# Masked cross-attention of a decoder: where the query projections and the token-gather masks stand in the instruction order

## The chip, the cores and the metric

The kernel runs on one core of one Trainium2 chip. The metric is the device time of one execution in microseconds. Before the change it is 1451.39 us, the median of three runs (1450.63 to 1454.59).

## The reference, cut to what matters

The reference is a decoder of two layers over 16 sequences of 128 tokens with 256 features. The change lies in the last attention and in the hand-over to the last feed-forward part (a mixture of eight experts, each of which picks the 32 tokens of a sequence that it scores highest):

```python
# masked cross-attention, 16 heads of 64
Q = (query @ W_q);  K = (key_value @ W_k);  V = (key_value @ W_v)
scores = jnp.einsum('bhmk,bhnk->bhmn', Q, K)
scores = jnp.where(mask == 0, jnp.float32(-1e+20), scores)
attn = jax.nn.softmax(scores / np.sqrt(D_K), axis=-1)
ctx = jnp.einsum('bhmn,bhnv->bhmv', attn, V)
x = _layernorm(x + ctx @ W_o)

# experts that choose tokens: E = 8, k = 128 // 8 * 2 = 32
affinity = jnp.transpose(jax.nn.softmax(jnp.einsum('bsd,ed->bse', x, gate_w)), (0, 2, 1))
gating, idx = jax.lax.top_k(affinity, k)
x_in = x[bidx, idx]
h = jax.nn.silu(x_in @ w_gate.T) * (x_in @ w_up.T)
x_e = h @ w_down.T
out = jnp.zeros_like(x).at[bidx, idx].add(gating[..., None] * x_e)
x = _layernorm(x + out)
```

## The kernel before, in words

All sixteen sequences stay in SBUF as tiles `x[b]`, 128 tokens by 256 features. The stages run one after the other; the masked attention is `stage4`, the experts are `stage5`.

`stage4` sets its order of work by hand: it opens a block with `manual_schedule`, and inside it every engine executes its instructions in the order in which the Python code issues them. The loop runs over the sequences, `for n in range(NB)` (L1936), and is a software pipeline. In iteration n the kernel makes the scores of sequence n in two halves of eight heads (`scores(n, 0)`, `scores(n, 1)`, L1827), the exponentials of n on ScalarE (`exp`, L1846), the division by the row sums on GpSimd after a reciprocal on VectorE (`weighted`, L1851), the transposes of the weights of n-1 in four pieces (`turn_weights(n-1, 0..3)`, L1855), each copied out of PSUM by `turned` (L1860: pieces 0 and 2 on ScalarE, 1 and 3 on VectorE), the product with the values for n-1 (`attend4`, L1863), and the output projection, residual and layer norm of n-2 (`product`, `residual`, `normed`).

Two sequences share one query projection. The queries of the pair g+1 are made during pair g: `queries(g+1)` is a generator of four pieces, each of eight matmul instructions in TensorE (L1747) and one evacuation on VectorE (L1752). An iteration takes two pieces, both directly behind `scores(n, 1)`. In odd iterations `turn(g + 2)` (L1811) transposes the input of the pair after that, which must follow the last piece that reads the one buffer `xT`.

Routing for the experts rides along. `r5.turn(n-3)` (L2075) transposes a finished sequence, ScalarE copies it out, and `r5.gauge(n-3)` (L2083) multiplies it with the gate weights. `r5.choose` (L2091) is a generator that turns the affinities of eight sequences into positions; for the first eight it is stepped through in iterations 11 to 13. `r5.take(b)` (L2136) then gathers the chosen tokens of one sequence: VectorE compares an index row with the positions and writes the 0/1 mask `hot` (L2125), TensorE multiplies `x[b]` with it, ScalarE copies the result to `xin`. Takes of sequences 0 to 7 come as fillers in iterations 13, 14 and 15 (L1910), those of 8 to 15 in a loop at the end of the stage (L2036). In iterations 0 and 1 the fillers are instead the last pieces of the keys and values (L1755, L1760), copied out by ScalarE.

PSUM limits this. `ps_t` (transposes and attention products) has two buffers, and `ps_m` (query pieces, `turn`, `product`, `r5.turn`, `r5.gauge`, takes, fillers) has two buffers. `hot` has two buffers in SBUF. `stage5` uses the same function `hot` with a pool of its own for the way back (`ways`, L2145); that stage has no order written by hand, and some of its mask instructions stand already inside iteration 13 in the trace.

The heart of the iteration before the change:

```python
scores(n, 1)
if g + 1 < NB // G:
    all_of(some(asked, g + 1, queries, 2))
if last:
    normed(n - 2)
if n > 2:
    r5.turn(n - 3, small, kv.ps)
if i == 1 and g + 2 < NB // G:
    turn(g + 2)
```

Of the kernel before, what the change touches and what calls it, by code (L numbers as in the profile page):

```python
# [8 lines left out]
F32 = mybir.dt.float32  # L9
# [11 lines left out]
NB = 16  # L21
# [1697 lines left out]
class Context4:  # L1719


    G = 2
# [59 lines left out]
def all_of(parts):  # L1782
    for _ in parts:
        pass


def stage4(K, w, kv, r5, res):
# [6 lines left out]
    with ExitStack() as ctx:  # L1794
        keep = ctx.enter_context(tc.tile_pool(name="s4_keep", bufs=1))
        grp = ctx.enter_context(tc.tile_pool(name="s4_grp", bufs=2))
        work = ctx.enter_context(tc.tile_pool(name="s4_work", bufs=2))
        small = ctx.enter_context(tc.tile_pool(name="s4_small", bufs=4))
# [8 lines left out]
        G = kv.G  # L1807
# [3 lines left out]
        def turn(g):  # L1811
            xT[g] = K.new(grp, [P, KD, G * P], F32, "xT", bufs=1)
            px = K.new(kv.ps, [P, KD, G * P], F32, "ps_m")
            for k in range(KD):
                for i in range(G):
                    nc.tensor.transpose(px[:, k, i * P:(i + 1) * P], x[G * g + i][:, k * P:(k + 1) * P], K.ident)
            nc.scalar.copy(xT[g], px)
# [6 lines left out]
        def half(b, j):  # L1824
            return s[b][:, 8 * j:8 * j + 8, :]

        def scores(b, j):  # L1827
            g, at = divmod(b, G)
            mine = slice(at * P, at * P + P)
            if j == 0:  # L1830
                s[b] = K.new(work, [P, NH, P], F32, "s")
            pss = K.new(ps, [P, 2, 4, P], F32, "ps_s")
            for c in range(4):
                for i in range(2):
                    rows = slice(64 * i, 64 * i + 64)
                    nc.tensor.matmul(  # L1836
                        pss[:, i, c, :], qT[g][j][rows, c, mine], kT[g][j][rows, c, mine], start=True, stop=True,
                    )
            nc.vector.tensor_tensor(  # L1839
                half(b, j), pss.rearrange("p r c k -> p (r c) k"), hide.unsqueeze(1).to_broadcast([P, 8, P]), ALU.add,  # L1840
            )
            m[j] = K.new(small, [P, 8], F32, f"m{j}", bufs=2)
            nc.vector.tensor_reduce(m[j], half(b, j), AX.X, ALU.max, negate=True)  # L1843
            t[j] = K.new(small, [P, 8], F32, f"t{j}", bufs=2)

        def exp(b, j, which):  # L1846
            for i in which:
                at = half(b, j)[:, i, :]
                nc.scalar.activation(at, at, AF.Exp, bias=m[j][:, i:i + 1], accum_out=t[j][:, i:i + 1])  # L1849

        def weighted(b, j):  # L1851
            nc.vector.reciprocal(t[j], t[j])  # L1852
            nc.gpsimd.tensor_tensor(half(b, j), half(b, j), t[j].unsqueeze(2).to_broadcast([P, 8, P]), ALU.mult)  # L1853
# [21 lines left out]
        def product(b):  # L1875
            py[b] = K.new(kv.ps, [P, D], F32, "ps_m")
            for c in range(NC):
                nc.tensor.matmul(py[b], oT[b][:, c, :], w.o[c // 4][:, c % 4, :], start=(c == 0), stop=(c == NC - 1))  # L1878

        def residual(b):  # L1880
            r[b] = K.new(work, [P, D], F32, "r")
            nc.vector.tensor_tensor(r[b], x[b], py[b], ALU.add)
            st = K.new(small, [P, 6], F32, "ln_st")
            nc.vector.bn_stats(st, r[b])
            mv[b] = K.new(small, [P, 2], F32, "ln_mv")
            nc.vector.bn_aggr(mv[b], st)
            rs[b] = K.new(small, [P, 1], F32, "ln_rs")
            K.rsqrt(small, rs[b], mv[b][:, 1:2], 1.0, 1e-5, "ln_t")

        def normed(b):  # L1890
            nc.vector.tensor_scalar(x[b], r[b], mv[b][:, 0:1], rs[b], ALU.subtract, ALU.mult)


        asked = {}

        def some(held, at, make, n):

            if at not in held:
                held[at] = make(at)
            for _ in range(n):  # L1900
                next(held[at])
                yield

        def fillers(n):
            if n < 2:
                for _ in range((3, 100)[n]):
                    if next(kv.rest, kv) is kv:
                        break
                    yield
            for b in {13: (0, 1), 14: (2, 3, 4, 5), 15: (6, 7)}.get(n, ()):  # L1910
                r5.take(b, small, kv.ps)
                yield

        H = NB // 2
        early, late = r5.choose(0, H, small, kv.ps), r5.choose(H, NB, small, kv.ps)
# [20 lines left out]
        for n in range(NB):  # L1936
            old, last = n > 0, n > 1
            g, i = divmod(n, G)
            parts = fillers(n)
            scores(n, 0)  # L1940
            exp(n, 0, range(8))
            if last:
                product(n - 2)
                residual(n - 2)
            scores(n, 1)
            if g + 1 < NB // G:
                all_of(some(asked, g + 1, queries, 2))
            if last:
                normed(n - 2)
            if n > 2:  # L1950
                r5.turn(n - 3, small, kv.ps)
            if i == 1 and g + 2 < NB // G:
                turn(g + 2)
            if n in (11, 12, 13):
                next(early, None)
            weighted(n, 0)
            exp(n, 1, range(0, 3))
            if old:
                turn_weights(n - 1, 0)
                turned(n - 1, 0)  # L1960
            next(parts, None)
            if n in (11, 12):
                next(early)
            exp(n, 1, range(3, 6))
            if old:
                turn_weights(n - 1, 1)
                turned(n - 1, 1)
            if n > 2:
                r5.gauge(n - 3, kv.ps)
            next(parts, None)  # L1970
            if n in (11, 12):
                next(early)
            exp(n, 1, range(6, 8))
            if old:
                turn_weights(n - 1, 2)
                turned(n - 1, 2)
            next(parts, None)
            if old:
                turn_weights(n - 1, 3)
                turned(n - 1, 3)  # L1980
            weighted(n, 1)
            next(parts, None)
            if old:
                attend4(n - 1, 0)
            all_of(parts)
            if old:
                attend4(n - 1, 1)
            if n == 12:
                next(early)

            if i == 1 and g + kv.ahead < NB // G:
                kv.fetch_keys(g + kv.ahead)
            if old and n - 1 + G * kv.ahead < NB:
                kv.fetch_values(n - 1 + G * kv.ahead)
            if n == 13:
                first = load5(
                    K, 0, lambda i, shape: K.new(kv.ring, [P, 4, 2 * P], F32, "ring").rearrange("p c n -> p (c n)")
                    if len(shape) == 2 else K.new(kv.ring, [P, 4, 2 * P], F32, "ring"),
                )


        b = NB - 1
# [31 lines left out]
        first_down(1)  # L2034
        all_of(late)
        for b in range(H, NB):  # L2036
            r5.take(b, small, kv.ps)
    return first


# [22 lines left out]
class Routes:  # L2063


    def __init__(self, K, pool):
        self.K = K
        self.gw = K.load(pool, "l1f_gate_wT", [P, KD, NE], rearr="(k p) e -> p k e", p=P)
        self.aff = K.new(pool, [P, NB, NE], F32, "aff")
        self.pos = K.new(pool, [P, NB, NE], F32, "pos")  # L2070
        self.xin = K.new(pool, [P, KD, NE, NB * TOK], F32, "xin")
        self.xT, self.back = {}, []


    def turn(self, b, work, ps):  # L2075
        K, nc = self.K, self.K.nc
        pt = K.new(ps, [P, KD, P], F32, "ps_m")
        for k in range(KD):
            nc.tensor.transpose(pt[:, k, :], K.x[b][:, k * P:(k + 1) * P], K.ident)
        self.xT[b] = K.new(work, [P, KD, P], F32, "xT5", bufs=2)  # L2080
        nc.scalar.copy(self.xT[b], pt)
# [43 lines left out]
    def hot(self, b, pool):  # L2125

        K, W = self.K, [P, NE, TOK]
        hot = K.new(pool, W, F32, "hot", bufs=2)
        K.nc.vector.tensor_tensor(
            hot, K.iota[:, :TOK].unsqueeze(1).to_broadcast(W), self.pos[:, b, :].unsqueeze(2).to_broadcast(W),  # L2130
            ALU.is_equal,
        )
        return hot


    def take(self, b, work, ps):  # L2136
        K, nc = self.K, self.K.nc
        hot = self.hot(b, work)
        pg = K.new(ps, [P, KD, NE, TOK], F32, "ps_m")
        for k in range(KD):  # L2140
            nc.tensor.matmul(pg[:, k, :, :], K.x[b][:, k * P:(k + 1) * P], hot, start=True, stop=True)
        nc.scalar.copy(self.xin[:, :, :, b * TOK:(b + 1) * TOK], pg)
# [214 lines left out]
```

## Time and profile before

| What | Value |
|---|---|
| median of three runs | 1451.39 us |
| the profiled execution's own time | 1454.16 us |
| its span in the profile | 1452.4 us |
| granted TensorE clock over the span | 0.951 |
| busy in the span: TensorE matmul, VectorE, ScalarE, GpSimd | 1271.0, 833.9, 647.7, 475.5 us |
| masked attention, first scores to the end of the last take | 787.5 to 1103.4 us |
| iterations 5 and 6 (an odd and an even one of the regular stretch) | 16.62 and 15.30 us |
| iterations 11, 12, 13, 14, 15 | 19.13, 17.70, 22.37, 19.10, 19.40 us |

Engine names in the views: PE is TensorE's matmul, PEld its weight loads, DVE VectorE, ACT ScalarE, POOL GpSimd. A line of the timeline has start, duration, engine, source line, operation, output and input tiles with shapes, a count when several instructions are merged, and in brackets the idle time of the engine before it with the instruction that ended this idle time. A line of the chain of waits has start, length and what the end of the program was waiting for in that time. A line of waits has the total in us, the times and the longest. Float32 matmuls are issued as two instructions each, so a query piece of four products shows as eight.

### The profile page before, as it was taken

What the parts mean: (1) busy time and instruction counts of PE and PEld (TensorE: products, weight loads), DVE (VectorE), ACT (ScalarE), POOL (GpSimd) and SP (SyncE); (2) the same over time, 40 slices, a digit from 0 to 9 for tenths busy, and PEclk for the clock granted to TensorE, in tenths of its full rate; (3) what the DMA queues carried; (4) which work ended last, traced back from release to release, by engine and by line L of the source; (5) the groups of instructions that cost most, each with busy time, mean ns of one, the idle gap of its engine ahead of it and who ended that gap; (6) DMA issues with size and microseconds to landing.
All of it is one profiled execution on the core that took longest, in us unless ns stands there. A gap on an engine that the chain in (4) does not pass through costs nothing.

```text
span 1452.4 us, 19245 instructions
## 1 busy us (share of the span) xinstructions
PE 1271.0 (88%) x6759; PEld 866.0 (60%) x6771; DVE 833.9 (57%) x1747; ACT 647.7 (45%) x1699; POOL 475.5 (33%) x627
## 2 busy tenths in 40 slices
PE   3688998889966899988998998988799999999995
PEld 1466544566653566656745777776677456666554
DVE  7898858889967676766745565566422411211115
ACT  6688854668954444432223555555532111111110
POOL 3266527657861654451033223322100200000003
PEclk9799998989998899998899999999999999999997
DMA  8376333201100000000100221211005112332102
GB/s 313 122 236 222 115 120 96 31 1 52 45 30 1 0 1 1 0 1 0 59 1 1 74 73 59 67 66 44 1 1 184 57 55 97 102 101 69 38 11 72
DMA packets 60272, 95.08 MB, mean 65 GB/s; under 512 B 11248, under 2 KB 40912, under 8 KB 59920
## 3 DMA queue, kind: packets, MB, share of 16 engines
q1 hardware_dynamic: 58000, 88.31, 18.2%
q0 software_dynamic: 2176, 5.55, 1.9%
q8 instruction: 53, 0.87, 0.3%
q14 instruction: 43, 0.35, 0.1%
HBM read 73.35 MB, written 16.29 MB: 62 GB/s over the span
## 4 chain that ended last, share of the span: by engine, by line
PE 63%; DVE 24%; POOL 4%; issue 4%; ACT 3%; DMA 1%; another core or an unknown queue 0%; SPq 0%; DVEq 0%; ACTq 0%; POOLq 0%
PE ps_y L2187 7%; PE ps_m L2176 7%; PE ps_g L2176 7%; PE ps_m L1878 4%; PE ps_m L1747 4%; PE ps_m L1290 3%; PE ps_t L1869 2%; PE ps_s L1836 2%; PE ps_y L1416 2%; PE ps_t L1858 2%; PE ps_k L1713 2%; DVE s L921 2%; PE ps_y L1396 2%; PE ps_seg L1358 1%; PE ps_m L1384 1%
## 5 line engine op out<-in xcount | busy, mean ns | idle before, releaser
L2181 DVE TENSOR_TENSOR h<-h,ps_m 128x512 f32<-128x512 f32 x60 | 41.3, 688 | 226.5 <-PE ps_m L2176 226.5
L82 POOL TENSOR_SCALAR ln_t<-ln_mv 128x1 f32<-128x1 f32 (+1 forms) x84 | 16.4, 195 | 446.8 <-DVE ln_mv L90 308.8
L1849 ACT ACTIVATE s<-s,m 128x128 f32<-128x128 f32 x256 | 99.3, 391 | 54.0 <-DVE m L1843 54.0
L2180 ACT ACTIVATE h<-ps_g 128x512 f32<-128x512 f32 x60 | 35.8, 597 | 171.6 <-PE ps_g L2176 171.6
L2176 PE MATMUL ps_g<-xin,w 128*128 128x512 f32 x224 | 106.2, 592 | 0.0
L2176 PE MATMUL ps_m<-xin,w 128*128 128x512 f32 x224 | 105.3, 592 | 0.0
L1853 POOL TENSOR_TENSOR s<-s,t 128x1024 f32<-128x1024 f32 x32 | 60.9, 1902 | 115.6 <-DVE t L1852 115.6
L2187 PE MATMUL ps_y<-w,h 128*128 128x256 f32 x448 | 97.8, 379 | 0.0
L2187 PEld LDWEIGHTS ps_y<-w,h 128*128 128x128 f32 x448 | 85.1, 190 | 14.6 <-issue 3.3
L933 ACT ACTIVATE s<-s,m 128x128 f32<-128x128 f32 x256 | 83.3, 394 | 17.4 <-DVE m L928 17.4
L2176 PEld LDWEIGHTS ps_m<-xin,w 128*128 128x128 f32 x224 | 42.5, 190 | 51.4 <-issue 50.2
L2176 PEld LDWEIGHTS ps_g<-xin,w 128*128 128x128 f32 x224 | 42.0, 190 | 46.4 <-issue 45.0
L1839 DVE TENSOR_TENSOR s<-ps_s,hide 128x1024 f32<-128x1024 f32 x32 | 39.2, 1224 | 42.7 <-PE ps_s L1836 42.7
L1747 PE MATMUL ps_m<-xT,half 128*128 128x256 f32 x256 | 59.5, 386 | 2.6 <-DVE qT L1752 1.9
L1878 PE MATMUL ps_m<-half,oT 128*128 128x256 f32 x256 | 59.3, 385 | 0.0
L1296 DVE SCALAR_TENSOR_TENSOR acc<-ps_m,l1a_conv_w,acc 128x508 f32<-128x508 f32 (+2 forms) x72 | 52.6, 735 | 11.0 <-ACT acc L1292 10.9
L2188 ACT COPY y<-ps_y 128x256 f32<-128x256 f32 x30 | 11.2, 373 | 104.7 <-PE ps_y L2187 58.5
L1747 PEld LDWEIGHTS ps_m<-xT,half 128*128 128x128 f32 x256 | 47.3, 190 | 10.7 <-DVE qT L1752 2.3
L1878 PEld LDWEIGHTS ps_m<-half,oT 128*128 128x128 f32 x256 | 47.4, 190 | 7.5
L83 POOL TENSOR_TENSOR ln_rs<-ln_t,mhalf 128x1 f32<-128x1 f32 (+1 forms) x84 | 48.8, 580 | 7.0
L1290 PE MATMUL ps_m<-xnT,l1a_in_proj 128*128 128x512 f32 x96 | 48.3, 629 | 1.6 <-DVE xnT L1281 1.5
L1849 ACT ACTIVATION_READ_ACCUMULATOR s<-s,m 128x1 f32 x256 | 48.4, 189 | 0.0
(503 smaller groups left out, 3118.9 us busy)
## 6 DMA issues: line engine op xcount, KB each, us to landing
w<-in_w_gate_dram SPq DMA_DIRECT2D x9, 1024.0 KB
w<-in_l1f_gateT_dram SPq DMA_DIRECT2D x14, 512.0 KB
w<-in_l1f_upT_dram SPq DMA_DIRECT2D x14, 512.0 KB
w<-in_l1f_downT_dram SPq DMA_DIRECT2D x14, 512.0 KB
k<-kv SPq DMA_DIRECT2D x20, 256.0 KB
v<-kv SPq DMA_DIRECT2D x20, 256.0 KB
ring<-k SPq DMA_DIRECT2D x10, 512.0 KB
ring<-v SPq DMA_DIRECT2D x10, 512.0 KB
```

The costliest lines, as they stand in the source:

```text
L83: return self.nc.gpsimd.tensor_tensor(out, t, self.mhalf[: out.shape[0], :n], ALU.pow)
L933: nc.scalar.activation(at, at, AF.Exp, bias=m[h][:, i:i + 1])
L1290: nc.tensor.matmul(pc, w.inp[:, k, at:at + P], xnT[g][:, k, :], start=(k == 0), stop=(k == KD - 1))
L1296: nc.vector.scalar_tensor_tensor(accv[:, :, j:], pcv[:, :, :P - j], w.conv[:, c, TAPS - 1 - j:TAPS - j], accv[:, :, j:], ALU.mult, ALU.add,)
L1747: nc.tensor.matmul(pq[:, j, :], wt[k][:, at], src[:, k, :], start=(k == 0), stop=(k == KD - 1))
L1839: nc.vector.tensor_tensor(half(b, j), pss.rearrange("p r c k -> p (r c) k"), hide.unsqueeze(1).to_broadcast([P, 8, P]), ALU.add,)
L1849: nc.scalar.activation(at, at, AF.Exp, bias=m[j][:, i:i + 1], accum_out=t[j][:, i:i + 1])
L1853: nc.gpsimd.tensor_tensor(half(b, j), half(b, j), t[j].unsqueeze(2).to_broadcast([P, 8, P]), ALU.mult)
L1878: nc.tensor.matmul(py[b], oT[b][:, c, :], w.o[c // 4][:, c % 4, :], start=(c == 0), stop=(c == NC - 1))
L2176: nc.tensor.matmul(ps[:, j, :], m[k][:, c * P:(c + 1) * P], self.r.xin[:, k, e, cols], start=(k == 0), stop=(k == KD - 1),)
L2181: nc.vector.tensor_tensor(h, h, pu, ALU.mult)
L2187: nc.tensor.matmul(pd, rows(c), w.down[c // 4][:, c % 4, :], start=(c == 0), stop=(c == FI // P - 1))
```

## The change

Four edits go together. The two query pieces of an iteration no longer stand together behind `scores(n, 1)`: the first stands behind `r5.gauge`, ahead of the third transposed piece; the second stands behind `weighted(n, 1)`, after the fourth transposed piece and ahead of `attend4(n-1, 0)`. `turn(g + 2)` moves behind the second piece. The mask `hot` is split from `take`: a new `want` makes it ahead, for sequences 2 to 7 before `scores(n, 1)` of iterations 14 and 15, for 0 and 1 ahead of `weighted(13, 0)`, and in the last loop one sequence ahead of its take. `hot` gets four buffers in place of two, in both stages that use it.

```diff
-            for b in {13: (0, 1), 14: (2, 3, 4, 5), 15: (6, 7)}.get(n, ()):
+            for b in taken.get(n, ()):
                 r5.take(b, small, kv.ps)
                 yield
+
+        taken = {13: (0, 1), 14: (2, 3, 4, 5), 15: (6, 7)}
...
+            if n > 13:
+                for b in taken[n]:
+                    r5.want(b, small)
             scores(n, 1)
-            if g + 1 < NB // G:
-                all_of(some(asked, g + 1, queries, 2))
+            more = some(asked, g + 1, queries, 2) if g + 1 < NB // G else iter(())
             if last:
                 normed(n - 2)
             if n > 2:
                 r5.turn(n - 3, small, kv.ps)
-            if i == 1 and g + 2 < NB // G:
-                turn(g + 2)
             if n in (11, 12, 13):
                 next(early, None)
+            if n == 13:
+                for b in taken[n]:
+                    r5.want(b, small)
             weighted(n, 0)
...
             if n > 2:
                 r5.gauge(n - 3, kv.ps)
+            next(more, None)
             next(parts, None)
...
             weighted(n, 1)
+            all_of(more)
+            if i == 1 and g + 2 < NB // G:
+                turn(g + 2)
             next(parts, None)
...
         for b in range(H, NB):
-            r5.take(b, small, kv.ps)
+            r5.want(b, small)
+            if b > H:
+                r5.take(b - 1, small, kv.ps)
+        r5.take(NB - 1, small, kv.ps)
...
-        hot = K.new(pool, W, F32, "hot", bufs=2)
+        hot = K.new(pool, W, F32, "hot", bufs=4)
...
+    def want(self, b, work):
+        self.hots[b] = self.hot(b, work)
+
     def take(self, b, work, ps):
         K, nc = self.K, self.K.nc
-        hot = self.hot(b, work)
+        hot = self.hots.pop(b)
```

More of the change, by code (lines that the diff above doesn't have):

```diff
@@ L2071, in __init__ @@
         self.xin = K.new(pool, [P, KD, NE, NB * TOK], F32, "xin")
-        self.xT, self.back = {}, []
+        self.xT, self.back, self.hots = {}, [], {}
     def turn(self, b, work, ps):
```

## The prediction

> **What bounds the kernel now.** I read the page first, then the chain of waits inside the masked attention, then the timelines of PE, ACT and DVE for one iteration, last the PE waits and the granted clock of short windows.
>
> ```profile
> PE 1271.0 (88%) x6759; PEld 866.0 (60%) x6771; DVE 833.9 (57%) x1747; ACT 647.7 (45%) x1699; POOL 475.5 (33%) x627
> ...
> PE 63%; DVE 24%; POOL 4%; issue 4%; ACT 3%; DMA 1%; another core or an unknown queue 0%; SPq 0%; DVEq 0%; ACTq 0%; POOLq 0%
> ```
>
> PE is the bound over the span. What the change can reach is therefore only the time in which PE waits inside the attention. The chain of waits over iteration 6, an even one:
>
> ```profile
> 882.92 1.09 PE ps_s L1836 x16
> 884.02 3.67 PE ps_m L1747 x16
> 887.70 0.69 DVE qT L1752
> 888.39 0.32 DVE x L1891
> 888.83 0.66 DVE s L1861
> 889.63 1.08 PE ps_t L1858 x8
> 890.73 0.70 DVE s L1861
> 891.48 2.00 PE ps_t L1869 x32
> ```
>
> The reader is to see two places where the chain leaves PE: ahead of the third transposed piece (889.63) and ahead of attend4 (891.48). Both wait for a copy of a transpose. Why the first is late is in the timelines of the same iteration:
>
> ```profile
> 885.32 1.22 DVE L1843 TENSOR_REDUCE m<-s 128x8 f32<-128x1024 f32 x1
> ...
> 887.92 0.37 ACT L2081 COPY xT<-ps_m 128x256 f32<-128x256 f32 x1 [2.79 <-PE ps_m L2079]
> ...
> 889.36 0.56 ACT L1861 COPY s<-ps_t 128x512 f32<-128x512 f32 x1
> ```
>
> The maxima for the second exponentials are ready at 886.54, yet ACT stands idle 2.79 us: the copy of r5.turn is ahead of them in its queue, and PE reaches r5.turn only after both query pieces. In the late iterations PE waits for masks (total, times, longest; then three of these waits):
>
> ```profile
> PE ps_m L2141 <- DVE hot L2129: 11.3, 7, 3.2
> ```
> ```profile
> 1010.48 1.57 PE L2141 MATMUL ps_m<-hot,x 128*128 128x256 f32 x4 [3.22 <-DVE hot L2129]
> ...
> 1025.65 1.13 PE L2141 MATMUL ps_m<-hot,x 128*128 128x256 f32 x4 [2.50 <-DVE hot L2129]
> ...
> 1044.75 1.76 PE L2141 MATMUL ps_m<-hot,x 128*128 128x256 f32 x4 [2.50 <-DVE hot L2129]
> ```
>
> And the clock (busy times by engine, then the granted PE clock, third column from the end):
>
> ```profile
> 973.00:975.00 2.00, 1.94 (x22) 1.94 (x24) 0.12 (x2) 0.23 (x1) 1.80 (x1) 0.61 0.00 0
> ...
> 991.00:993.00 2.00, 2.00 (x24) 2.00 (x22) 1.93 (x3) 0.43 (x1) 1.58 (x1) 0.50 0.00 0
> ```
>
> After the idle places of iterations 11 and 12 PE runs at about half clock: attend4 takes 3.37 and 3.59 us there against 2.00.
>
> [...] Here a mask took 0.37 to 0.43 us alone, but three took 2.79 us from 1004.87 while GpSimd divided weights. [...]
>
> **The regular iterations, 2 to 10.** S is the start of scores(n,1), 882.85 in iteration 6. From S to the next iteration's start is 10.56 us in an even one (893.41 - 882.85) and 11.88 in an odd one (iteration 5: 878.11 - 866.23). The 4.74 us before S are untouched. Prices, start to start in the PE timeline: scores half 1.10, query piece 1.78 (3.55 for two), r5.turn 0.22, two transposed pieces 0.88, gauge 0.44, turn 0.50, attend4 1.93.
> New order after S: scores to 1.10, r5.turn to 1.32, pieces 0 and 1 to 2.20. The xT copy follows the last exp of the first half, which ends at 885.13, so it ends at S+2.56; gauge 2.60 to 3.04; first query piece to 4.82. DVE: maxima end at S+3.69, as now; normed (0.32) and the reciprocal (0.12) follow, turned 1 ends at S+4.74, which with the 0.15 us seen between such a copy and PE gives the third transposed piece at 4.89. ACT: first exp at S+3.78 (0.09 after the maxima, as for the first half); turned 0 begins 1.17 us later, as now, and ends at 5.51; fourth piece 5.60 to 6.04. Second query piece to 7.82; it hides turned 3 (a 0.69 us DVE copy). Turned 2 ends on ACT 4.14 us after the first exp (888.19 to 892.33 now), at 7.92, before the second half of attend4 needs it at 8.79. Next iteration at 7.82 + 1.93 = 9.75. **Even: 0.81 gained.** In odd ones turn adds 0.50: 10.25 against 11.88, **1.63 gained**; there the xT copy of turn no longer stands ahead of the exponentials. Iteration 2 has no r5.turn and ends at the same chain: 9.92 against 9.75, 0.17. Sum: 0.17 + 4 x 0.81 + 4 x 1.63 = **9.9 us**.
> The qT copies move behind turned 1 and behind the second reciprocal in DVE's queue; their readers come an iteration or more later, and they end ahead of the next scores' addition (S+11). They cost nothing; without that cover a copy would be 0.69. No DMA is moved: the SP queue's fetches stay behind the iteration, and GpSimd's first division only starts earlier.
>
> **Iterations 0 and 1** (a loss). Now both query pieces come first and cover the softmax of the first sequence. Moved, piece one of the keys stands at once behind the scores; its ACT copy waits behind the exponentials and ends near 8.66 after the iteration's start (last exp of three ends at 795.67 now). The two ps_m buffers then block PE from 5.5 to 8.7. Iteration 0: 8.7 + two fillers of 1.73 + query piece 1.78 = 13.95 against 12.09. Iteration 1 by the same steps, filler at 9.15, about 15.9 against 15.31. Together 2.5, and idle places of 3.2 and 2.7 us invite the half clock, at 1.6 each if it comes (3.59 - 2.00 above): between 2.5 and 5.7, I take **-4.5**.
>
> **Iterations 11 to 15 and the takes.** 11: choose puts the affinity exponential and two small steps ahead of the second exponentials; PE then waits until about S+7.1 for the transpose of affinities; end at 12.3 against 14.38, less 1.6 if the half clock stays: 0.5 to 2.1, I take 0.6. 12: end at 10.55 against 12.75, same doubt: 0.6 to 2.2, taken 1.4. 13: masks ready at S+4.9, but stage 5's own masks stand in DVE's queue here; four buffers and GpSimd's two outputs would let six in where four came, and turned 1 and the gauge copy queue behind them. End between 13.5 and 16.6 against 17.63: taken 1.5. 14: four wants, 4 x 0.40 = 1.6 us on DVE ahead of scores' addition, delay maxima, exponentials and everything behind them on ACT and DVE by that; the second take waits to 6.4 for a buffer; end 12.0, or 13.5 at half clock, against 14.36: taken 0.9. 15: two wants, 0.8; end 10.6 to 11.7 against 14.66, which held half clock: taken 3.0. Sum **7.4**.
> **The last loop and stage 5.** The loop runs 32 matmuls in 7.41 us and is paced by ACT's copies; earlier masks save 0.3. Stage 5's masks are paced by DVE (1.66 us per two, 0.60 copy and 1.06 masks); two made earlier save about 0.5, bounds 0 and 1.1. Taken **0.8**.
>
> **Sum.** -4.5 + 9.9 + 7.4 + 0.8 = 13.6. The profiled execution took 1454.16 (span 1452.4 and 1.8 around it), 2.8 above the median of the runs: 1440.6 for it, **1438 us** for the median. The later stage is bound by PE, so the gain is carried to the end.
>
> **Rivals.** (a) PE never falls to half clock in the new places: about 8 us more (2.0 at the start, 1.6, 0.8, 1.5, 1.5 and 1.0 in 11 to 15), 1429 rounded. For it: the regular iterations' 1.3 to 1.8 us of idle time leave the clock at 1.00; against it: 11's 2.8 us did not. (b) The PSUM buffers of transposes are freed in the other order, the third piece waiting for ACT's turned 0, the fourth behind it: 0.44 more in 11 iterations, 4.8: 1443, and to 1446 with more half clock. Iteration 2 shows that order, 3 to 10 the one that I use. (c) **Slower:** the third and fourth pieces do not come earlier, since the exponentials of the second half, not the query pieces, hold turned 0; then the queries only move from a covered place to behind the transposes. Even: third at 6.78 as now, both done at 7.66, query piece 9.44, attend4 11.37, a loss of 0.81; odd about 0.6; over 12 iterations 8.5, with the 4.5 above less some 5 from the takes: 8 slower, 1459. It decides from the point where the fourth piece starts later than S+6.4 (10.56 - 1.93 - 1.78 - 0.44); I have 5.6. Against it: maxima at S+3.69 do not depend on the queries. (d) The masks' delay and the start eat the gain: 1451.
>
> **Chances.** Forecast 0.50 (its own range 1432 to 1444), (a) 0.17, (b) 0.15, (d) 0.07, (c) 0.11. A measurement tells about 0.3%, 4.4 us, from no change. Faster 0.82, same 0.07, slower 0.11. The range 1427 to 1447 leaves out (c), (d) and the edge of (a).
>
> **What would show it.** Right: ACT's idle place ahead of L2081 gone, exponentials of the second half 3.8 us after S, even and odd iterations near 14.5 and 15.0 us, iteration 0 longer, the 2.50 waits for hot gone. Wrong: the third or fourth transposed piece after S+6.4, or a clock below 1.00 in iterations 2 to 10.

## The result, and the profile after

The changed kernel takes 1428.76 us, the median of four runs (1424.18 to 1433.79), against 1451.01 for the kernel before (four runs): a ratio of 0.9869, 95% interval 0.984 to 0.9898. That is faster by 22.3 us, clear of the 0.3% that a measurement tells. The forecast was 1438, with a range from 1427 to 1447.

The profiled execution took 1424.18 us, with a span of 1422.5. It is 29.9 us shorter than the span before, but 7.3 of these lie ahead of the attention, which begins at 780.19 here and at 787.51 before, in code that the change doesn't touch; over all profiles of this study that start lies between 780 and 794 us. So I compare stretches inside the attention, and not whole spans.

The page's first line shows where PE stands now; its busy time fell by 11.4 us from the 1271.0 above with the same 6759 matmuls. At half clock the same work is busy for longer (attend4 took 3.59 us in iteration 12 before, 2.00 in iteration 6), and the granted clock over the span is 0.962 here and 0.951 before; that this is the whole of the 11.4 us is not shown:

```profile
PE 1259.6 (89%) x6759; PEld 853.6 (60%) x6771; DVE 831.5 (58%) x1747; ACT 646.6 (45%) x1699; POOL 475.9 (33%) x627
```

PE's timeline over iteration 6, from scores(6,1) to attend4, the stretch that the chain showed before:

```profile
871.99 1.16 PE L1836 MATMUL ps_s<-ring,qT 64*128 64x128 f32 x16
873.08 0.44 PE L2091 MATMUL ps_m<-ident,x 128*128 128x128 f32 x2
873.36 1.04 PE L1858 MATMUL ps_t<-ident,s 128*128 128x128 f32 x8
874.58 0.61 PE L2099 MATMUL ps_m<-l1f_gate_wT,xT 128*128 128x8 f32 x4 [0.19 <-ACT xT L2093]
875.05 1.97 PE L1747 MATMUL ps_m<-xT,half 128*128 128x256 f32 x8
876.86 1.29 PE L1858 MATMUL ps_t<-ident,s 128*128 128x128 f32 x8
877.99 1.89 PE L1747 MATMUL ps_m<-xT,half 128*128 128x256 f32 x8
879.81 1.97 PE L1869 MATMUL ps_t<-s,ring 128*64 128x128 f32 x32
```

The reader is to see that no bracket stands ahead of the third piece (876.86) or of attend4 (879.81): a query piece lies ahead of each, and only 0.19 us ahead of the gauge is left. The ACT side of the same iteration (VectorE's maxima, then ACT's copy of r5.turn and the first exponential behind it):

```profile
874.46 1.22 DVE L1843 TENSOR_REDUCE m<-s 128x8 f32<-128x1024 f32 x1
```
```profile
874.18 0.35 ACT L2093 COPY xT<-ps_m 128x256 f32<-128x256 f32 x1
875.71 0.40 ACT L1849 ACTIVATE s<-s,m 128x128 f32<-128x128 f32 x1 [1.19 <-DVE m L1843]
```

The copy is done before the maxima are, and the exponentials begin 0.03 us after the maxima end; before, ACT stood idle until PE had come through both query pieces. In the late iterations the waits for masks have become fewer, and others took their place (PE's waits over the whole attention: total, times, longest, the first line from before the change and the others changed; then PE's timeline in iterations 13, 14 and 15):

```profile
PE ps_m L2141 <- DVE hot L2129: 12.1, 8, 3.2
```
```profile
PE ps_m L2156 <- DVE aff L2100: 4.2, 2, 2.4
...
PE ps_m L2156 <- DVE hot L2141: 3.2, 2, 2.4
```
```profile
983.84 1.87 PE L2156 MATMUL ps_m<-hot,x 128*128 128x256 f32 x4 [2.43 <-DVE hot L2141]
...
1005.29 1.13 PE L2156 MATMUL ps_m<-hot,x 128*128 128x256 f32 x4 [2.41 <-DVE aff L2100]
...
1021.16 1.71 PE L2156 MATMUL ps_m<-hot,x 128*128 128x256 f32 x4 [1.74 <-DVE aff L2100]
```

The 12.1 us of waits for masks over the attention before are 3.2 now. The second take of iterations 14 and 15 waits instead for a ps_m buffer that the gauge's copy on VectorE frees.

Iteration by iteration, from the starts of scores(n,0) in PE's timeline (the last row but one runs from the end of iteration 15 to the first experts' matmul behind the last take, the last from there to the end of the transposes of the way back):

| stretch | before, us | changed, us |
|---|---|---|
| 0, 1 | 12.09, 15.31 | 13.12, 15.21 |
| 2 | 14.66 | 14.46 |
| 3 to 10, odd / even | 16.62 / 15.29 | 14.90 / 14.46 |
| 11, 12 | 19.13, 17.70 | 18.95, 14.96 |
| 13, 14, 15 | 22.37, 19.10, 19.40 | 20.16, 16.55, 16.20 |
| rest of the attention | 48.42 | 46.74 |
| first part of stage 5 | 32.96 | 32.27 |

The attention as a whole, first scores to that experts' matmul, is 315.85 before and 293.81 changed; with the 0.69 of stage 5 the change is worth 22.7 us in the profiles, which agrees with the medians.

### The profile page after: what moved, and what is told of

Its sections match the earlier page's. It is cut to its first block, busy times and chain, and to the rows that moved or that the text cites. A ratio compares the mean times of both kernels' runs of the same rounds, so it can differ in the third digit from the quotient of the medians.

```text
span 1422.5 us, 19270 instructions
## 1 busy us (share of the span) xinstructions
PE 1259.6 (89%) x6759; PEld 853.6 (60%) x6771; DVE 831.5 (58%) x1747; ACT 646.6 (45%) x1699; POOL 475.9 (33%) x627
## 4 chain that ended last, share of the span: by engine, by line
PE 63%; DVE 22%; ACT 6%; POOL 4%; issue 3%; DMA 1%; SPq 0%; DVEq 0%; ACTq 0%; POOLq 0%
PE ps_y L2202 7%; PE ps_m L2191 7%; PE ps_g L2191 7%; PE ps_m L1747 4%; PE ps_m L1290 3%; ACT s L1849 2%; PE ps_t L1869 2%; PE ps_m L1878 2%; PE ps_seg L1358 2%; PE ps_y L1416 2%; PE ps_k L1713 2%; PE ps_y L1396 2%; DVE s L921 2%; PE ps_m L1384 2%; PE ps_m L1767 1%
## 5 line engine op out<-in xcount | busy, mean ns | idle before, releaser
L933 ACT ACTIVATE s<-s,m 128x128 f32<-128x128 f32 x256 | 83.2, 393 | 16.9 <-DVE m L928 16.7
L1747 PE MATMUL ps_m<-xT,half 128*128 128x256 f32 x256 | 63.0, 391 | 2.6 <-DVE qT L1752 1.9
L1350 POOL TENSOR_TENSOR run<-upper,da 128x1024 f32<-128x1024 f32 x16 | 30.7, 1924 | 52.5 <-DVE da L1342 30.7
```

The source lines that it names most:

```text
L933: nc.scalar.activation(at, at, AF.Exp, bias=m[h][:, i:i + 1])
L1747: nc.tensor.matmul(pq[:, j, :], wt[k][:, at], src[:, k, :], start=(k == 0), stop=(k == KD - 1))
```

## The experiments

"Attention" below is that same stretch, before 315.9 and changed 293.8. Ratios are against the kernel before.

**Only the queries.** The moved query pieces and the moved turn, with masks and buffers as before.

```diff
-                all_of(some(asked, g + 1, queries, 2))
+                more = some(asked, g + 1, queries, 2)
...
+            next(more, None)        # behind r5.gauge
...
+            all_of(more)            # behind weighted(n, 1), then turn(g + 2)
```

> Only the query pieces and turn(g+2) are moved; masks are made inside take with two buffers, as before. Theory (the moved pieces fill two gaps of TensorE, masks do the late part): iterations 4 to 10 at 14.5 us (even) and 14.9 us (odd) as in the changed kernel, iteration 0 near 13.1, iteration 12 near 15.0, iterations 14 and 15 as before at 19.1 and 19.4; the attention from its first scores to the first experts' matmul behind the last take 301 to 304 us against 315.9 before and 293.8 changed. Rival (the masks are what counts, the queries only move the waits): iterations 4 to 10 above 15.2 and 16.4, attention above 310.

Measured: 1438.19 us, ratio 0.9901 (0.9866 to 0.9936). Regular iterations 14.46 and 14.90 us, iteration 12 14.96, 14 19.10, attention 302.6. Iteration 0 took 14.81, not 13.1, at a mean clock of 0.88. But for that miss the theory holds, and the rival falls.

**Only the masks.** The wants and four buffers, with the queries in a block behind the scores as before.

```diff
+            if n > 13:
+                for b in taken[n]:
+                    r5.want(b, small)
             scores(n, 1)
...
-        hot = K.new(pool, W, F32, "hot", bufs=2)
+        hot = K.new(pool, W, F32, "hot", bufs=4)
```

> Only the masks are made ahead, with four buffers in both stages; the query pieces stand together behind the scores as before. Theory: iterations 2 to 12 as before (15.3 and 16.6), 14 and 15 near 16.6 and 16.2 as in the changed kernel, 13 between 20 and 21.5, attention 306 to 310 us; the first part of stage 5 about 0.7 us shorter than before (37.3 against 37.95). Rival (masks ahead help only together with the queries): 14 and 15 above 18.

Measured: 1442.4 us, ratio 0.9928 (0.99 to 0.9957). Attention 307.1, iteration 13 20.98, first part of stage 5 32.27 (32.96 before). Iteration 14 took 17.97 where 16.6 was expected; its mean clock was 0.90 and that of the changed kernel's 1.00. Iteration 15 took 15.20 at full clock, a microsecond less than expected. So the rival (both above 18) falls by 15, and 14 stands at its edge. The regular iterations stayed at 15.3 and 16.6, except for one at 18.08 with a clock of 0.91. The two halves gain 13.3 and 8.7 us of attention, and the whole change 22.0: they add, although half clock fell in other places in each profile (the last section has the sum without it).

**Only r5.turn first.** Does freeing ACT's queue do it, or the work in the gaps?

```diff
             scores(n, 1)
+            if n > 2:
+                r5.turn(n - 3, small, kv.ps)
             if g + 1 < NB // G:
                 all_of(some(asked, g + 1, queries, 2))
             if last:
                 normed(n - 2)
-            if n > 2:
-                r5.turn(n - 3, small, kv.ps)
```

> Only r5.turn is moved ahead of the two query pieces, which stay together, so that ScalarE's copy of it no longer holds the exponentials. Theory (TensorE needs work between the transposes; freeing ScalarE alone is not enough, as piece 1 is transposed late and its copy on VectorE still ends 0.85 us after it): even iterations 15.0 to 15.3, odd 15.9 to 16.3, attention 310 to 314 us. Rival (the gain is ScalarE's freed queue): even 14.5 to 14.7, odd 14.9 to 15.2, attention 303 to 305.

Measured: 1444.92 us, ratio 0.9965 (0.9951 to 0.9979); even 14.83, odd 15.90 (one odd iteration, at a clock of 0.91, 17.30), attention 306.7, below the range expected: its profile spends three times 3.41 us at half clock in the attention, the one before six times. PE's timeline in an even iteration:

```profile
884.64 1.17 PE L1858 MATMUL ps_t<-ident,s 128*128 128x128 f32 x8
886.60 1.97 PE L1869 MATMUL ps_t<-s,ring 128*64 128x128 f32 x32 [0.78 <-DVE s L1861]
```

Freeing ACT closes the gap ahead of the third piece, which I had not given it: the even iterations gain 0.46 us and fall below my 15.0. The 0.78 ahead of attend4 stands exactly as before, since it is the time of turned 3 on VectorE after the fourth piece; only work put there can hide it. So my theory is right for the gap ahead of attend4 and was wrong for the other, which ScalarE's freed queue closes alone; the rival (14.5, the whole gain from that queue) falls.

**Only the second piece.** The first query piece stays behind the scores.

```diff
+                more = some(asked, g + 1, queries, 2)
+                next(more)
...
+            all_of(more)            # behind weighted(n, 1), then turn(g + 2)
```

> The second query piece and turn(g+2) are moved ahead of attend4, the first piece stays behind the scores; masks as before. Theory: the gap ahead of attend4 is filled, the one ahead of the third transposed piece stays by about 0.4 us: even 14.8 to 14.9, odd 15.3 to 15.4, iteration 0 near 12 to 12.5. Rival (both pieces must be moved, since the third transposed piece starts no earlier than before): even above 15.2, odd above 16.2.

Measured: 1441.97 us, ratio 0.9924 (0.9901 to 0.9947); even 14.97, odd 15.40, iterations 0 and 1 12.23 and 13.57. PE's timeline:

```profile
890.53 1.06 PE L1858 MATMUL ps_t<-ident,s 128*128 128x128 f32 x8 [1.08 <-ACT s L1861]
...
893.25 1.97 PE L1869 MATMUL ps_t<-s,ring 128*64 128x128 f32 x32
```

The gap ahead of attend4 is gone, that ahead of the third piece grew to 1.08, waiting for turned 0 on ACT. So the second piece alone gives 0.32 us (even) and 1.22 (odd) of 0.83 and 1.72. The first two iterations are together 2.5 us shorter than in the changed kernel; for iteration 0 that was expected, for iteration 1 not. In odd iterations this run also moves `turn(g + 2)`: they gain 0.90 us more than the even ones here, 0.89 in the changed kernel, and only 0.26 in the run above, where `turn` stays behind the scores. So most of the odd iterations' extra gain comes with moving `turn`, but no run moved it alone.

**Masks an iteration earlier.** In the changed kernel, wants for 14 and 15 at the end of 13 and 14.

```diff
-            if n > 13:
-                for b in taken[n]:
-                    r5.want(b, small)
             scores(n, 1)
...
+            if n in (13, 14):
+                for b in taken[n + 1]:
+                    r5.want(b, small)
```

> The changed kernel with the masks for iterations 14 and 15 made at the end of iterations 13 and 14, behind the second query piece's place, and not ahead of the scores' addition. Theory (four masks ahead of the addition delay the maxima, and through ScalarE's queue the copies that free TensorE's buffers): the wait of 2.4 us ahead of the second take of iteration 14 falls to about 1.0, iteration 14 near 15.2 us against 16.55, from the first scores of iteration 15 to stage 5 1 to 1.7 us less than 62.9, iteration 13 within 0.5 of 20.2. Rival (the wait is for the second take's buffer, whatever stands ahead of the maxima): 14 stays at 16.3 to 16.7.

Measured: one profiled run, 1432.77 us. Iteration 14 15.33, iteration 13 20.14; the wait ahead of the second take:

```profile
1013.85 1.13 PE L2156 MATMUL ps_m<-hot,x 128*128 128x256 f32 x4 [1.19 <-DVE aff L2100]
```

2.41 became 1.19: four masks ahead of the scores' addition did hold PE, by way of the maxima and VectorE's queue. From iteration 15 to the experts' matmul it took 63.1, as much as the changed kernel's 62.9 and not 1 us less: iteration 15 itself was shorter (14.65 at full clock), but half clock came in the rest (0.96 over 48.4 us, against 1.00).

**choose later.** Steps two and three of choose in iteration 11 behind the fourth piece and behind the second query piece.

```diff
-            if n in (11, 12):
+            if n == 12:
                 next(early)         # both places between the transposes
...
+            if n == 11:
+                next(early)         # behind turned(n - 1, 3), and again behind turn(g + 2)
```

> The changed kernel with the second and third step of choose in iteration 11 moved behind the fourth transposed piece and behind the second query piece. Theory (iteration 11 is long because the second step waits for ScalarE's affinity exponential ahead of VectorE's copy of piece 1, TensorE idles 2.3 us and falls to half clock for a while): iteration 11 15.2 to 15.8 us against 18.95, 12 as before at 15.0. Rival (choose's own work is what costs): above 17.5.

Measured: one profiled run, 1426.12 us. Iteration 11 took 16.40 against 18.95, which is 0.6 us above the range expected. Of these 2.55 us, 1.7 is half clock that did not come (the changed kernel's second profile has 17.27 there at full clock), and only 0.9 the wait itself. But iterations 13 and 14 took 21.50 and 18.01, and the attention 296.0, 2 us more than in the changed kernel. What was saved in 11 came back as half clock elsewhere.

**Iteration 13's masks earlier.** The last step of choose and two masks ahead of product(n-2).

```diff
             exp(n, 0, range(8))
+            if n == 13:
+                next(early, None)
+                for b in taken[n]:
+                    r5.want(b, small)
             if last:
                 product(n - 2)
...                                  # the old places of both go
```

> The changed kernel with the last step of choose and the two masks of iteration 13 put ahead of product(n-2), where VectorE waits for TensorE. Theory (the first take waits 2.4 us for a mask that queues behind the scores' addition and maxima, and the half clock follows): the first take no longer waits for its mask, iteration 13 17.5 to 19 us against 20.2; stage 5's masks now fall among the residual's and the scores' steps, about 2 us ahead of the maxima, and keep it above 17. Rival (stage 5's masks ahead of turned 1 set iteration 13, wherever the first take stands): 19.7 to 20.7.

Measured: one profiled run, 1432.26 us. Iteration 13 took 18.37 us against 20.16, and the first take has no wait, as expected. But PE waits behind it instead:

```profile
993.44 1.99 PE L1747 MATMUL ps_m<-xT,half 128*128 128x256 f32 x8 [2.67 <-DVE aff L2101]
```

The clock in iteration 13 was 1.00 here and 0.92 in the changed kernel. A fall to half clock cost about 1.7 us in iterations 0 and 11 (last section), so all but 0.1 of the 1.79 us are half clock that did not come, and the masks' place gave next to nothing. Iteration 14 took 18.01 at a clock of 0.91. Attention 293.4.

**Four buffers in stage 4 alone.** `take`'s masks with four, the way back with two.

```diff
-        hot = K.new(pool, W, F32, "hot", bufs=4)
+        hot = K.new(pool, W, F32, "hot", bufs=bufs)    # 4 from want, 2 from ways
```

> The changed kernel with four mask buffers in stage 4 and two in stage 5, as before the change there. Theory: from the first experts' matmul behind the last take to the end of the transposes of the way back 32.9 to 33.0 us as before the change, against 32.3 changed; iteration 13 0.2 to 0.6 us shorter than 20.2, with four masks of stage 5 in it and not six; the rest alike. Rival (more buffers in stage 5 do nothing): 32.3 and 20.2.

Measured: one profiled run, 1432.53 us. The first part of stage 5 took 32.96, as before the change: its 0.69 us are the buffers' own. Iteration 13 took 20.14 and not less; that four of stage 5's masks, not six, stand there changes nothing.

**The combination,** timed beside the changed kernel in five rounds: the first query piece behind the scores in iterations 0 and 1, masks an iteration earlier, choose later.

```diff
+            if n < 2:
+                next(more)          # directly behind scores(n, 1)
...
-            next(more, None)
+            if n > 1:
+                next(more, None)
...
                                     # and the edits of masks an iteration earlier, choose later
```

> The changed kernel once more, timed beside the two that follow. Expected 1424 to 1434 us, ratio to the kernel before 0.984 to 0.990; regular iterations 14.46 and 14.90 us; the attention 293 to 297 us, depending on how many times TensorE falls to half clock (1.7 us each).

> The changed kernel with three edits: in iterations 0 and 1 the first query piece stands behind the scores again (as in the run that moved only the second piece: 12.2 and 13.6 us against 13.1 and 15.2), the masks for iterations 14 and 15 are made at the end of 13 and 14 (15.3 us against 16.6 for 14), and steps two and three of choose in iteration 11 come later (16.4 or less against 17.3 to 19). Theory: the savings add, attention 286 to 290 us against 294 to 296, total 1419 to 1426 us, ratio 0.979 to 0.985. Rival (half clock comes elsewhere for each wait removed): attention above 292, ratio as the changed kernel's.

> As the combined kernel, and the last step of choose with the masks of iteration 13 ahead of product(n-2), which gave 18.4 us for iteration 13 against 20.1. Theory: attention 284 to 289 us, 1.5 to 2 us below the combined kernel's, total 1417 to 1425 us. Rival (what is saved in 13 returns as half clock in 14): as the combined kernel.

| kernel | median, us | ratio to before (95%) | attention, us |
|---|---|---|---|
| changed, again | 1425.88 | 0.9835 (0.9806 to 0.9865) | 293.9 |
| combined | 1423.61 | 0.9809 (0.9779 to 0.9840) | 285.9 |
| combined, and 13 earlier | 1425.96 | 0.9824 (0.9793 to 0.9856) | 289.0 |

In the profile the combination's savings add, 8.0 us of attention: 4.2 in iterations 0 and 1, 0.9 in 11, 1.2 in 14, 1.7 in 15. Of the 4.2, 1.7 is half clock that stood in iteration 0 of that profile of the changed kernel (14.81, not 13.12); the edit's own share is 2.5, as in the run of only the second piece. The 1.7 in 15 are half clock too (a clock of 0.90 there, 1.00 here); it came in none of the three profiles with the masks an iteration earlier. By its median it is the fastest kernel of the study, but its interval overlaps that of the changed one, so it is not shown to beat it. The third kernel is no better: its attention is 3.0 us longer, all of it between the end of iteration 15 and the experts' matmul, where the clock was 0.93 and not 1.00, and its iteration 13 took 20.05. PE's timeline there, a query piece behind the wait for a buffer, at half clock:

```profile
987.64 3.66 PE L1747 MATMUL ps_m<-xT,half 128*128 128x256 f32 x8 [2.67 <-DVE aff L2108]
```

The same piece takes 1.97 us elsewhere. The rival holds, though in iteration 13 itself and not in 14 (15.32 us): the wait saved ahead of the take stands ahead of the query piece, as it did in the run that moved only these masks (2.67 us in both), and this time half clock came with it.

## Why the prediction was right, and where its sizes were off

The direction, the mechanism and the range were right; the gain of 13.6 us was too small. By the terms of the sum:

| term | forecast | profiled |
|---|---|---|
| iterations 0 and 1 | -4.5 | -0.9 |
| iterations 2 to 10 | 9.9 | 10.4 |
| iterations 11 to 15 | 7.4 | 10.9 |
| last loop and stage 5 | 0.8 | 2.4 |
| sum | 13.6 | 22.7 |

**Regular iterations.** The forecast was right step by step. Even 14.49 us forecast, 14.46 measured; odd 14.99 and 14.90. In iteration 6 S is 871.99: gauge at S+2.59 (2.60 forecast), third piece at 4.87 (4.89), second query piece at 6.00 (6.04), attend4 at 7.82 (7.82). The qT copies, costed at nothing, cost nothing: no wait of PE in these iterations ends with one. Buffers came free in the order that I used, VectorE's first, so rival (b) did not come. Rival (c) fell, since the fourth piece stands ahead of the second query piece and so well ahead of S+6.4. The experiment with r5.turn alone shows that the exponentials do come earlier when r5.turn no longer stands behind the queries, and the one with the second piece alone what a late turned 0 costs: 1.08 us ahead of the third piece.

**Iterations 0 and 1.** This term was mis-sized. I let the second filler wait for the buffer of the first, which ACT's copy frees. In the trace it takes the buffer of the query piece, which VectorE frees earlier (PE's timeline of iteration 0):

```profile
787.95 3.70 PE L1767 MATMUL ps_m<-l1x_W_v,ctxT 128*128 128x512 f32 x8 [2.05 <-DVE qT L1752]
```

The wait is 2.05 and not 3.2 us. For the transposes I had used the rule that the buffer that is free first is taken; here I went by turns. And I charged 2 us of half clock: this profile has none in iteration 0, others do (14.81 in the changed kernel's second profile, at 0.88). Of the seven profiles with this start (the changed kernel's two, and five of runs that keep it), five show 14.8 and two 13.1, so -2.6 is the more frequent value. It changes nothing in the sum: where iteration 0 has the half clock, iteration 11 has none (14.81 and 17.27 in the changed kernel's second profile, 13.12 and 18.95 in its first), and the two terms together are -0.8 us in both.

**Iterations 11 to 15.** The waits were where I had put them, and half clock was charged in the wrong places. 11 waits 2.33 us for the affinities' transpose (2.3 forecast) and then runs at half clock: 0.2 gained, 0.6 forecast. 12 and 14 ran at full clock where I had counted 0.8 and 1.5 us against them: 2.7 gained for 1.4, and 2.55 for 0.9. In 13 six masks of stage 5 stood in VectorE's queue where four had stood, as forecast, and four of them took 3.92 us while GpSimd divided for 1.90 of it; 2.2 gained for 1.5. 15 gained 3.2 for 3.0. The delay of the maxima by wants in 14 was real: moving it away took 1.2 us off.

**Last loop and stage 5.** Stage 5 gave 0.69, within its bounds and shown by the buffers' own run. The loop itself gave nothing: 32 matmuls in 7.41 us, as before. But 1.68 us came from a hidden-layer block of 16 matmuls ahead of it, 5.38 us before and 3.70 changed, one passage at half clock that did not recur. That term was not in my sum.

The median came out at rival (a)'s 1429, but only in part by its cause: no half clock came in iteration 0 of this profile (2.0 charged), in 12 (0.8) and in 14 (1.5), but it did come in 11, 13 and 15. Of the 9.1 us by which the sum was short, 4.3 are these three charges, 1.7 the hidden-layer block and 1.6 the shorter wait at the start; a few tenths each make up the rest. That this adds up to (a)'s figure is chance.

One reading was too simple. The prediction put half clock down to the idle places ahead of it. But in the 3.42 us ahead of iteration 12's fall before the change (987.08 to 990.50) PE was busy for 1.72, and its longest wait there was 0.96 us.

What stays open: how to place the half clock. The last section shows at which times it began in two traces, 3.41 us or a multiple apart, but no run here controlled where the attention starts between such times.

## What to carry to other kernels

When an engine in order waits for a copy of what it has just made, independent work that stands elsewhere in the same iteration can fill the gap at no price (here it took 0.83 us off an even iteration), as long as its own readers are far off and its evacuations don't stand ahead of the copy. Follow each gap to its releaser first: here one was a late queue entry, and reordering that entry alone closed it (0.46 us); the other was a plain round trip (0.78 us) that closed only when work was put there. Masks and other small inputs made ahead are worth having, but not in front of the reduction on which the iteration's longest chain hangs (in iteration 14 four masks there cost 1.2 us).

## What the runs showed of the hardware that I had not expected

PE fell to half clock without any long idle gap. In iteration 12 before, its two waits were 0.96 and 0.78 us, yet the clock went to 0.50; in the regular iterations of that profile, with 1.3 to 1.8 us of waits in 15 to 17, it stayed at 1.00. A fall cost about 1.7 us here: iteration 0 is 13.12 or 14.81, iteration 11 17.27 or 18.95, in the two profiles of the changed kernel.

The clock records of two traces, of the kernel before and of the changed one, show when the falls came there. In each trace the starts of all its stretches of half clock (24 before, 19 changed) lie 3.41 us or a multiple of it apart, to within 3 ns; those inside the attention last 3.41 us, but for one of 6.83 before. I call these 3.41 us a step; why the starts lie so is not shown. Here are steps of the changed kernel in iterations 0 and 11, and one of its second profile in iteration 0, each with the step behind it (PE's busy time is the first after the length; the clock is third from the end):

```profile
786.06:789.47 3.41, 1.52 (x4) 0.81 (x5) 0.96 (x3) 3.41 (x18) 1.90 (x1) 1.00 0.00 0
789.47:792.89 3.42, 3.42 (x13) 2.07 (x12) 0.20 (x1) 2.36 (x9) 1.25 (x1) 1.00 0.00 0
949.90:953.31 3.41, 1.08 (x9) 0.77 (x8) 3.31 (x7) 3.41 (x17) 1.83 (x1) 1.00 0.00 0
953.31:956.73 3.42, 3.42 (x11) 2.79 (x10) 0.80 (x2) 0.65 (x3) 1.84 (x1) 0.50 0.00 0
```
```profile
790.65:794.07 3.42, 1.38 (x3) 0.68 (x4) 1.12 (x3) 3.42 (x18) 1.85 (x1) 1.00 0.00 0
794.07:797.48 3.41, 3.41 (x5) 1.35 (x4) 0.20 (x1) 1.92 (x9) 0.66 (x2) 0.50 0.00 0
```

The attention starts 0.95 us into a step in the first profile and 1.11 us in the second. With the same instructions in the same order, PE is busy for 1.52 us of the step at 786.06 in the first and for 1.38 of the one at 790.65 in the second, and only in the second does half clock follow. Iteration 11, with the same wait of 2.3 us, falls in the first profile and not in the second, where iteration 0's 1.7 us had moved everything behind it; that this move is the cause is my reading of the two profiles.

Over 320 us from the attention's start the two traces hold 181 steps at full clock, 89 before and 92 changed. The four in which PE was busy least, 0.50 to 1.09 us, were all followed by half clock. Of the 16 with 1.52 to 2.29 us four were, and of the 161 with 2.39 us or more none. So in these traces half clock came behind steps with little work, but the busy time alone doesn't tell: a step with 1.52 us was followed by full clock, one with 1.99 us by half. This is a count of what was seen; no run was made to test it.

Between the first scores and the experts' matmul six steps ran at half clock before the change, three in the changed kernel, five with only the queries and four with only the masks. By an estimate from the 1.7 us of iterations 0 and 11, at most 5.1 of the 22.0 us gained there are half clock that went away; without it the halves give 11.6 and 5.3 us, and the whole change 16.9. The same order of instructions gave both values in iterations 0 and 11, so a single profile misjudges an edit of 1 to 2 us in such an iteration.
